# Fewer slots per expert, a down projection with tokens as rows, one relu for two chunks, and a new order, in a routed mixture-of-experts kernel

## The chip, the cores and the metric

The kernel runs on one core of a Trainium2 chip. The metric is the time in device microseconds of one execution; lower is better. Engines are named as in the profile: PE multiplies matrices (PEld is its loading of the stationary operand), DVE is the vector engine, ACT the scalar engine, POOL the general one, SP only starts DMAs. PSUM is the memory that PE writes to; it has eight banks of 512 fp32 columns.

## The reference

The input is 16 sequences of 256 tokens with 128 features, 4096 tokens in all. Four layers follow each other, each added to its input after a layer norm.

```python
x = x + attn_a(layernorm(x), ...)    # its softmax sums to one over keys that v does not depend on:
                                     # what is left is (x @ wv.T + bv) @ wo.T + bo
x = x + ffn(layernorm(x), gate_w, w1, w2)
x = x + attn_b(layernorm(x), ...)    # a selective scan with 16 states
x = x + ffn(layernorm(x), gate_w, w1, w2)
```

The feed-forward layer is a mixture of 8 experts with two chosen for each token:

```python
gate_logits = x @ gate_w
top_vals, top_idx = jax.lax.top_k(gate_logits, 2)
top_w = softmax(top_vals)
h = relu(einsum('td,edf->etf', x, w1))          # d = 128, f = 512
expert_out = einsum('etf,efd->etd', h, w2)
final = sum of the two chosen experts' rows, weighted by top_w
```

All data are fp32.

## The kernel before

The tokens are cut into eight blocks of 512. For each of the two feed-forward layers the blocks are grouped in sets: `FIRST` is block 0, block 1, and the pairs 2-3, 4-5 and 6-7; `SECOND` is the pairs 0-1, 2-3 and 4-5, then 6 and 7 alone. A set is routed (`route`, L1133): each chosen row is scaled by its weight and written by an indirect DMA on POOL (`scatter`, L851) to a slot in DRAM that belongs to its expert. `SLOTS` (L32) says how many slots an expert has: in layer 1 192 for a single block and 330 for a pair, in layer 2 216 and 384. If some expert gets more rows than that, a flag is set and the function `general` computes everything again after the main part, without routing.

`experts` (L1183) then works through the eight experts of a set, one tile each. A tile of N slots is C times K rows, C = 2 for single blocks and C = 3 for pairs. For each tile:

- SP fetches the rows (`xs`), PE transposes them in C products against `ident`, and a copy on ACT or DVE brings them to SBUF as `xsT`, 128 features by N tokens.
- Up: four products with chunks of `w1` as the stationary operand and `xsT` streaming, N columns each, into PSUM banks of the kind "b". For single blocks two chunks share a bank (`pair`) and one relu takes both to `h`; for pairs each chunk has a bank and a relu of its own.
- Down: four products with chunks of `w2` stationary and `h` streaming, N columns each, summed in the one bank of the kind "y" (`py`). The result has features as rows. It is copied out (`yT`), transposed back by PE in C products into a "b" bank, copied out again (`yr`) and written to DRAM (`ys`).

`collect` (L1230) gathers the two rows of each token with indirect DMAs on POOL (`gather`, L863) and adds them. Behind layer 1 `mixer` (L1274) computes the selective scan for one or two blocks at a time. It puts its broadcast products into PSUM banks of the kind "B", each as wide as two banks, in which DVE also works in place. `BANKS` (L48) divides the eight banks: five "b", one "y" and one "B" (which counts twice).

All of this is first noted as jobs in a `Plan`. `Plan.forward` places the jobs one by one on the engines by assumed durations; a job that can run on ACT or DVE goes where it starts first, and among jobs that could start at the same time a rank decides, which is read from the string `ORDER`. The instructions are issued in the resulting order, so each engine's queue is fixed in advance and is worked off strictly in that order.

Where the plan has PE idle before a job, the kernel puts idle products there, on a block of zeros (L1488, named ps_y<-blank,ones_d in the profile): one for each 0.24 us of planned idle time, unless a sum in the "y" bank is under way (`summing`). They write to columns of the "y" bank that the tiles do not use. `WARM` limits them to jobs that start before a given time; at 1e6 all jobs do.

Most operations are recorded by one helper, so they have its line, L752, in the profile and are told apart by their tiles. In the profile `w_s` stands for both expert weights: ps_b<-xsT,w_s is an up product, ps_y<-h,w_s a down product. An fp32 product leaves two records, a transpose or a bf16 product one.

Of the kernel before, what the change touches and what calls it, by code (L numbers as in the profile page):

```python
# [19 lines left out]
P = 128  # L20
L = 256
TB = 512
# [9 lines left out]
SLOTS = ((192, 330, 480, 632), (216, 384, 600, 800))  # L32
# [3 lines left out]
WARM = 1e6  # L36
# [11 lines left out]
BANKS = dict(b=5, y=1, B=1)  # L48

ORDER = (  # L50
    "c-l=@2Ow4N8$RdUd&!70vKq1ql~8D@C{dE^GTPA|XlN%R<0l~`5)BE}Pef!SDI=1MG^Bx$k&1iI_<!Gbu73Zn?!D*SZ@l00KJW8B"
    "=S$_1jb!(<qPM-{q&;qMY=SG3cUzS|l8Uq$KUFJ5{S?3EP+zs^os@%5+Gjc2Nq>t9JMzFH%-zB#Ja4nYlf+G$9mW!_B}u0Tn@;cy"
    "9=$jIA+D3ZPjji7tiV5OuUk;*?O$*8qLrzu-V$N+=g3<+pZ`!Jx9QgD!1?BB)t9awRXc6A>8lL0BHpk?^H9z0Zq9<&1B#*wt}!bF"
    "<MdrQn+&dtG+zEKcE);Je%;`<#9N1QgKD&G6_YFD^(u8neD7yjo>LELnfk;)O7lpdNYUauW!dKG>eDNej5Y_9Tyiaar{|HlPdVx1"
    "PKim`3Ho`%YwSAe65bcO&C1KJSbgmZaVW0nprAi2K0QifduD!wxIRy^gfd;<aY1p~l5Ix~f6Cn)_6)Q$+&g1N<iWx9ev_<3>(Z^>"
    "b>*4(&bE;XZ17OM5`N?SvH|f;AC{ghnRM!M_o`iAJDrOo?;iGgR`739>V@?(YHpR&o(~HwuRK>OTlvWEORwX&ROZ4m3(e2o$_wcq"
    "C(fFT?by&g_r`8n@46kO3InGCiZ(6zGbUwj*XwfMM^THv{JhJ|>xpA3lV6SzAK9WE-LCNF&I;Fi-H`)}8YGt)R7R#68HdDV+Sbip"
    "`RkdKktpZu_ZLnF$9ErYa)=(;>a!<#`HbR2j#;gr4y}xzUlXsNbm<j6P$k(vH~1>w`<Bk+HgDszOUF*{R6jCD=G8SHs_EF0fVZ`2"
    "-66f-6Q>?M5*jxxyko8RO{Zx--;y#?>eNCKoOQn`|E|+B<e#5WsuHa4{b-E?SDrjmN*PgQ+H3M0eO5_67`k<=wy_}U$4Y&El=ovT"
    "I&#qVK+h%XFQxzHZ?WJEmU+~c4uq)Xo_E{)=+n(HyV8pLy0xWbdGlJu)3<B%+@GcBJbvc=G(T&}X~&vH<n9N!Hq33G&|`aet~ygC"  # L60
    "ni9HTK;^S(Pjk~LXDUA{A);*6oSX;E?HaK^7U^m9$wfs@3nC43))gfYV>8{}99nMt>)fBdhE?}-)3iz^YcJFInEkx^aCiLUm0ItX"
    "|8rc~$XdJE>Z80uM&g)63&~lPi+370RcjbaoD6h7FnoPXrb(yW-Q$e)&`VLS^jJF;QzP?-;a62#PaL{Xv9$X9w+}bE;_F2tcUlKL"
    "v^*esrGMGn$4uIZ%8%C*zI-bFR9RW96t3dhW<G5NcVYj_Wr|Hd{%Pf>{~I!y8&E#0`IFAVWj-^$=Vs52ob2hgYLKs%-)$V6<g(*s"
    "RsMJFt*4Lf{}r22=}7!E|NLv+JUV#qL-SL7>pkV<3Wpm%&KB$&mVYdNQla3qme{kSizatgOeBWvzb_nfZsSD3Th7v_LsvB06pbzP"
    "xaDU(YO)-=y)KvNO1-=0vZ$64t1SM0M#A<spXes^7S{PDG@g8akt>T&UFq8qc;Vuor0a5Ok0Qh+$9q{9D>q5l&94n_9y(n9D8-=8"
    "bz*9q+t#q18{I!#+U;X;9COOQu4lLILe0f5gFWiU4&gE8Ez)Y&hsSwl9ZNF}<&h?LaNX{%Rgds<Iol?v=WpwO5|v>o8ry0U;O=-B"
    "OD>q(x6<XXhKIkOl8(mWe;gd^6?eY;JSlj-p#g2#>#|M!&>{K#>i%^_6V*>%?s13|FU-q1(rkWhO4Gfv+p7*-qheY=J~3^07vVR{"
    "q%06KxgXr<;fve++1YT`BhXG)S>#^a3!mZu9X@Y?&TW798^3;qbbc5SeD-=c+4y(z@(-O7&2c+#N@_olIv8(1^YGWaXGg=TbX8S*"
    "pOi)!@{|U9CYo$<nCtM}vdPpz<sG@fH*n2}_{PBrb98QO%1q1S{cf(V575~c6LKZJaO}AapLd6>mp55Duh004nWwYu=jn2(;+yU}"
    ")t833zENM1P_K8_i}rJHUAOncEc@ujsPwhY_3EMuDq|g0t~=jM4q~>(HknU%Fc@dGC1mkcLWet7)N8+U`h@D~A62FHXi!}(O6~i@"  # L70
    "=C8TY;`O3ac@L-jSmdTO$qujXY)Sl?(fK2LfB!4p=@&Z3<84r3#rDHJvsd2i?B5__=5TtvwEFR54SJRmCZTh@2TkW4Xjgi7<KpgO"
    "PG5>>e3g7-Os1$}?vbO>#*bpABrJB-_(Q#ENZ;_GN+(ETe?(r*bM1F0&0V!54wD}%dX?5kmf41IHcz(<7?^2`zqv9r_FTuEo0)bW"
    "x(B?aHAlXAE67dTyfjv!ciM*Ag<iA2M2z|JSnA)>@#WI}{JcJ$TeZRdwPg!D-R-9KX)0v-`RTM(%H8~$R^_PR@3%BTZHk^@M&6Rp"
    "ts<dyF|LWdeZ}#sF0NM#d#!O*_Dthz<)mEoPiKbf&**Dk`<mZgEwg=J>g;7=bdy#r_qJ&4pjk`+m73Dtzu8H3U#R47*%KWP{c|kD"
    "9nW7?lhFHlzvx2TKfyhB3;uarYg5;e(|$Fqc~WG8t5u9liOLO$+Lo27_F-!Y>4F6d%F}*Kd*-<1nJ9iPp*+Yc@li@|<i1N2V&l?Z"
    "-<nRlS*ge8+qX8_<v*SJL%-rvhi9$z8TXT?a`3d%%8R!ppA&m|J#xwZ33oKg;|E_I=%e=*8$PKCi!nSjJ?_3lfzfU8v%~ao*shr$"
    "45Y7r(dv6&K4){A=-A!FEx-1T%b(H~t5v#B7Wv+mRPN$)DOB$0i=+p3Pdu!qR9LN8``~Q&*6(ulOy#D?2B+iU14}ZQ6<yZdPdK3!"
    "a&Ff`GCPWP8(H(OO_aS;^2=$yjGfNrngsd#RzpiFPxmHvkqa(A9x}9Xm6uW)v7goJJ9u?q_TA))H>Km!9g=dHD1QmbhLT#-`MgA<"
    "Xzv%{yIf4Aj`;9q$;KM+ibCmqEz?`D+N*IFw@(yp7*4ln*g2_uxl*Xl`Or4X>rJ2D)Wk`p{+krEv(GQTxk~QGw6bo8AIa(3iiL&B"
    "?<4D%yfY7xX}>shPrN5vY+8+sAl}Po#K`S=h<D3ex4;+GuMO(#7QYHiKB+X+B{pft^S847=b8h3bw0l<8RHr8q$FEnP5Qk<7IW|J"  # L80
    "y`Hi1_`gOWeNKVPPPfUVWa9<vZa0?n1$C+pF8cJT#zjRzAmiHHv>{2vRof=UeR-FSjfi~ixUA(Q{z3HN+x7jSM_jkvz_lLBNJS6D"
    "C4}93qhFz`DPpRq?_n2iw9P0(XW^aQ#{;X?+N8qTa$C1ZNWH%t!b=g!m3&yd#>VjNg97j8TV_1IQlYxp#A)xP@xAxs_Id~kUoBX5"
    "A+u#(f@W0ooIR%$w`(ud9a@%^yyR<GbMp1ak>xf4St)1VxmC0gmQC|4TEzJEWd}@4$z$1_UngHHv1K$ZR==uj+-&St`Sr>6^p8nJ"
    "GRyW~QJuYSrdYX=rRD@1&47kKRfP_38t;tdXC>;UH#zq`x^UR@WJGCC_z`_eL#10%IrBTpPKwsVh@39lDi>a`r7_`!1ukwD_xXC?"
    "^8T(lm_@DCvGoJBjfxzu!lq|hu@#q@^^F^6_lF<6n_1=M6EUkK+HwBMu-9Qvbt@tq`S!meAL`M3^AkJcr&jdWXm^CH`ZitQZhL;x"
    "whL=>DtbN+tnmtY5ODg8wX#S-nyh(Yhb`AA=SZ}=SwusmbJF@LyCR!o=KRT0dA;OB$30nx*t#upHZ`Xrzl9zQ+u17ND{nvFUh}x@"
    "S$%5QL-O1n`Rq>*B!Zsg7FeoHkSoJma(jo~jKA9Ds!epRw3r#}B1VfZ92>j(ta5N!QG}u~Caxa#r=ir@ct&2*E59(ejS1WZy~WFZ"
    "st?LdnJ|)QrgKWLAzFNgqs7ODpKErhybw<v^VDP3*Sc~$`)0|zB^rel*<~;GoXwWk*HGMh+e}gG;O|?i^%>U%_D>U43Qt~WHXEM6"
    "P3R6K+v@Km$#~{0HpFK+jL+E~=<3E7+21N_X|B7X*wWsU_h7S0<r&ZYZBh%fd|o(})>pmT;`hEfuY2B8g~w5`X(D#pzs>JWOEy3G"
    "<;F_eEgR?LFlUcm%MV#0yLFylWZ$%%_jV_@Txct?dv;D%?t1#~<F$RMt;>HkzwkQX)K;}EZ9$QD`?sJs_oT;M{1pDCMDQSMMeedk"  # L90
    "?qzAN+2s<4>aA9ni>dNc_I^^xsChPdz$-MP?t`xF<2W)P^M#6=-N+8rAI=$ujj`=To4rzd6HG13ou@c=iG9DcT2nOo)9w7_&z9S3"
    "=v*A3W{SH^-jLAxdYXdV*(X&|mIvx{qSasQ-86sE*Gs-7vlLS{)t_$P-{Sh>i?N|@cYDxkeCmQ9k(LHE1?Tr^wth4@JY>aP`!#ql"
    "IABYKN$)d-!{5XX$k^1)JXCgo2-)6MmTUN}wapM;IjrO!I}mij*=hcWMNj9HUv6nfkEBjadhL71CJkGlQI-CdKj+zmAv`nV;?xSF"
    "=;zx@at0>SJ!$7FhwgoiBRPw2IyRb3m~u0!{Zx%vc=(b~0pWdW?XE#<C;#q<tb)d*yi;;Bc8uj%9L(ub+Mj6k#?B?9Dm%zQPN#Iy"
    "f-O4LTFn=ST@2OT{BvG@n^3<_Ki1`Nj&k*MYx(2pKFU#kHNL@of9pX@&(v$>hjDZJvMpaN-v^w!VZBzbim_HyHs~A{|M2UCe3#L<"
    "GdsGK8aW=)Roj2w;TJ2a`H9EK@YeP<&2dSqjC!atRCo8I%c9Rq-FxDrZmGH#Jy7uTXq)%k*CN-g*Y~Y6esEPre4mEv#0ajg)1{;9"
    "Ok&>E?OopxlrqJ1cx#WYyOg4W<GQF{Jej)p*Pg#pi=RjtX?T*6tAA%tty5}$u-LCX-1MpcRngelWfj4q*^i4Wo@Q0J99Pze(_dAX"
    "eq-#8e=R$+cS~*+UwJP?W3~jxVvD;{VbWr|m<tI{6{^fqo1#<gd^+8ZDFwzH`R14GrsyxN)w;BNL?Q9L{o13;AI@!FZflz{G9lOO"
    "rF*B;ddt@{`W)O}S?A~}v=Gw2<iZLj1?UJ2f+pRop4@QcjQ1`3{H<dat4`T-ZI_nLyXxr+YuC-(NZy?lJ$$uG&Cq{e)}{}>(oGMQ"
    "Yq`taug*_W4)#p<)KlG=qG8Xwz9;Hc(1Lii&z|WNuivlI%jnwEqn}?-9m$+|t=u)~r*cB7&&J%`hzC2@h*v%TZT@`symM`C$q8Rf"  # L100
    "%<ih#*xF#HRF69!thVaOoY-+;#^=l@&cwNBv-${monOI^cN&?}uRb1cF?`W`+QGT>d7E_Ud7D!Q{rXmkth>soX}wq=b#zdb$E_Bd"
    "jtd9@{b!Kwm+kqkAd!*zt?`V6-TUc@dz}<o6|5u*l4bvJsXbZ({Z_|5k=Nv~v64i$C_Tgrb8$C|%H6EV*)cC)h7;+{h>T11e?B0k"
    "%vVTDI3f}=Yj)`Z7dhu<kA{Ep3f&tV%q@3kj4Tp0Z11g@D{Ih4gt}1aoCa#0%)~2|Lmh5voaQsScU#r9OvUcR1jedj7{-7Xcn2Ri"
    "fe|D|(gY1|P&h{56pe96hQ=`(qX-U#;RH?5I0FXLU^qjgd2l`$!(cdgLu1jR!as)HfZYXN;}}liI0d$12)GcKzz`H1!U5ZXJGgKH"
    "`oq~};0Ff;M$;e&QIZf46ptApK$J9k!3Y?3Ul=}3z<t0!lAypP+M2`Xk{He5gDn{x4rbu0H2g|{2yhx6j9|cu7#IOJgFnH^;1i4h"
    "GvH4I7%l+g;DNa$h=wFk>;f1B*bL0UF@^wf&<q3#r#S+K;Xphw2rtd0z<m-U2r!ocUr`W3cqoW1Lvb-&0KdRnw5Wi@DF6@xnBssi"
    "!6jH5=g<trgS&#?g#b_l8;=02N)X@}B$tBdf}aIA7bb=T0D!r0Bd`d97@nE|34sZ~afaf6O$opPuoxHu2I2q<uqxP9fHNGN53mCG"
    "fH*O91+qqfW0IICDd6&PoLvy12m*rOF^E7gRFFOdJpdO(1}Ff?z#xPXSPViNk%~ZkA}ID?U=+NMk1`G%kAlI&SiycIj)PQ#RSBBM"
    "P~Zsg9H8O|NC^_)iipT#0Pb)TFbO1y#9<C#o*<}T1b_+VkW14X6h00ECUK1AABD;S@)fK}!N4H%*!Urpa1<E^KXKv@TnQjSViX62"
    "&Ij{BsF1$|%reX-1tR7UfS@pYU}*}#5Az3UA%I6kj6@V+na$FKL0@nbF)h4iP|YC}VX!c3G+T0P{h`XkQ7&0P+4>az7ZxTw1kH|R"  # L110
    "OOA#Nh5Q7`qF`AvkRS})6;KJWUH}q}(nGT`pc;VNu)9N)5iXE&*r*WD1iLMRgaqdz5}=Z05eJabC`gP8K}P7n`h(&F$Og&@q!%aQ"
    "Vk9blhNgHFikrkq4k#@KvJ5A1Buot2nJp2799#789l#Bdg5)FMnE}f=NE9#u2jUBf4^;uk23UrI709B8L$ZLMIA}?D79eI6&1Fvn"
# [102 lines left out]
class Plan:  # L215
# [79 lines left out]
    def forward(self, rank):  # L295
# [33 lines left out]
        for _ in range(n):  # L329
# [38 lines left out]
            for table, s in ((j.after, done + HOP), (j.next, t)):  # L368
                for a in table:
                    when[a] = max(when[a], s)  # L370
                    left[a] -= 1
                    if not left[a]:
                        offer(a)
# [1185 lines left out]
```

## Time and profile before

| | |
|---|---|
| median of 6 runs | 688.06 us (680.34 to 690.06) |
| the profiled execution | 689.38 us |
| its span, first to last instruction | 687.7 us |
| PE busy | 569.8 us, 2928 records |
| DVE, ACT, POOL busy | 331.0, 327.8, 323.7 us |
| mean granted PE clock | 0.919 |
| up and down products | 211.1 and 226.6 us, 640 records each |
| idle products | 71.3 us, 526 records |
| indirect DMAs on POOL | 128 scatters of 980 ns and 128 gathers of 974 ns |
| DMA traffic | 55.09 MB, 80 GB/s on average |

The chain of waits is followed back from the last instruction: at each step to what released it. A line of the groups gives the engine, the operation, what it writes and reads, the shape, the count, then the busy time, the mean of one, and the idle time of the engine before it with what ended it. Matmuls are pipelined: the duration of one record is longer than the distance to the next, so that the cost in a dense stretch is read from one start to the next.

### The profile page before, as it was taken

Reading aid. Unit: us, or ns where it says so; the run is one execution under the profiler, and the core shown is the slowest. Engines: PE = TensorE matmul, PEld = TensorE weight load, DVE = VectorE, ACT = ScalarE, POOL = GpSimd, SP = SyncE. Lnnn points to the kernel's source line nnn. Section 1 sums busy time; section 2 is a strip of 40 time slices with the busy share of each in tenths; the row PEclk is TensorE's granted clock in tenths of the full one; section 3 lists DMA queues with packets and bytes.
Section 4 is the critical chain, followed back from the end, with each engine's and each line's share of the span. In section 5 each row is a group of like instructions: output and inputs, shape, how many; then the busy total and the mean of one; then the engine's idle time right before and its main releaser. Section 6 shows DMA issues by size and latency. Waiting matters only on the chain.

```text
span 687.7 us, 9182 instructions
## 1 busy us (share of the span) xinstructions
PE 569.8 (83%) x2928; PEld 416.6 (61%) x2928; DVE 331.0 (48%) x1073; ACT 327.8 (48%) x795; POOL 323.7 (47%) x451
## 2 busy tenths in 40 slices
PE   7988987686988797969987898998479939887695
PEld 7988976554656474636654454654246626686585
DVE  4736543233577456748766675776253512101010
ACT  1223653333777445748566676874134523343130
POOL 3266154545437456373847384316705563244413
PEclk9999998978999789989999999999779978898799
DMA  8933121322023111321233123202333132232211
GB/s 248 294 119 115 40 66 42 98 75 68 26 86 93 35 44 51 100 69 33 69 99 90 33 66 92 59 28 80 84 89 92 38 101 63 90 95 58 68 61 47
DMA packets 76375, 55.09 MB, mean 80 GB/s; under 512 B 8064, under 2 KB 69152, under 8 KB 76320
## 3 DMA queue, kind: packets, MB, share of 16 engines
q1 hardware_dynamic: 66464, 37.35, 18.6%
q0 software_dynamic: 8192, 16.79, 8.4%
q8 instruction: 25, 0.41, 0.3%
q10 hardware_dynamic: 1664, 0.29, 0.2%
q14 instruction: 30, 0.25, 0.1%
HBM read 27.09 MB, written 27.32 MB: 79 GB/s over the span
## 4 chain that ended last, share of the span: by engine, by line
PE 72%; another core or an unknown queue 8%; ACT 7%; issue 7%; DVE 4%; POOL 0%; DVEq 0%; ACTq 0%; POOLq 0%
PE ps_b L752 40%; PE ps_y L752 23%; PE ps_y L1488 7%; PE ps_B L752 2%; ACT decay L752 1%; ACT h L752 1%; ACT th L752 1%; ACT L752 1%; ACT row L752 1%; DVE w L752 1%; DVE ps_B L752 1%; ACT yr L752 1%; ACT yT L752 0%; DVE xn L752 0%
## 5 line engine op out<-in xcount | busy, mean ns | idle before, releaser
L752 PE MATMUL ps_y<-h,w_s 128*128 128x330 f32 (+3 forms) x640 | 226.6, 450 | 18.2 <-issue 8.7
L752 PE MATMUL ps_b<-xsT,w_s 128*128 128x330 f32 (+3 forms) x640 | 211.1, 449 | 30.8 <-ACT xsT L752 12.6
L863 POOL DMA_INDIRECT yy<-ys,of x128 | 124.7, 974 | 121.9 <-issue 60.9
L851 POOL DMA_INDIRECT slots<-row,to x128 | 125.5, 980 | 103.8 <-issue 32.8
L752 PEld LDWEIGHTS ps_b<-xsT,w_s 128*128 128x128 f32 x640 | 120.3, 206 | 77.0 <-issue 21.1
L752 ACT ACTIVATE h<-ps_b 128x384 f32<-128x384 f32 (+2 forms) x209 | 99.0, 481 | 105.0 <-PE ps_b L752 67.1
L752 PEld LDWEIGHTS ps_y<-h,w_s 128*128 128x128 f32 x640 | 111.9, 205 | 52.6 <-issue 20.1
L1488 PE MATMUL ps_y<-blank,ones_d 128*128 128x128 f32 x526 | 71.3, 287 | 10.8 <-POOL ones_d L752 4.0
L1488 PEld LDWEIGHTS ps_y<-blank,ones_d 128*128 128x128 f32 x526 | 66.0, 200 | 14.6 <-issue 4.5
L752 PE MATMUL ps_b<-ident,yT 128*128 128x128 f32 (+3 forms) x208 | 47.8, 290 | 24.7 <-ACT yT L752 21.6
L752 ACT COPY yT<-ps_y 128x384 f32<-128x384 f32 (+3 forms) x62 | 25.0, 403 | 73.1 <-PE ps_y L752 36.2
L752 POOL TENSOR_TENSOR rstd<-var,root 128x8 f32<-128x8 f32 (+1 forms) x20 | 29.9, 1494 | 54.7 <-DVE var L752 49.6
L752 PEld LDWEIGHTS ps_b<-ident,yT 128*128 128x128 f32 (+3 forms) x208 | 27.3, 143 | 41.3 <-ACT yT L752 25.0
L752 DVE TENSOR_SCALAR h<-ps_b 128x330 f32<-128x330 f32 (+2 forms) x47 | 24.4, 524 | 55.7 <-PE ps_b L752 45.9
L752 ACT COPY yr<-ps_b 110x384 f32<-110x384 f32 (+3 forms) x57 | 24.6, 431 | 50.9 <-PE ps_b L752 31.5
L752 DVE TENSOR_TENSOR ps_B<-du,ps_B 128x224 f32<-128x224 f32 (+15 forms) x55 | 22.0, 400 | 43.8 <-remote 14.0
L752 PE MATMUL ps_b<-ident,xs 110*128 110x110 f32 (+3 forms) x208 | 40.5, 276 | 2.1 <-issue 1.1
L752 ACT ACTIVATE th<-later,lneps,ha_s 128x112 f32<-128x112 f32 (+13 forms) x85 | 39.1, 504 | 0.0
L752 PEld LDWEIGHTS ps_b<-ident,xs 110*128 110x128 f32 (+3 forms) x208 | 28.1, 149 | 13.8 <-issue 6.0
L752 DVE BATCH_NORM_STATS2 stats<-x 128x6 f32<-128x128 f32 x128 | 28.9, 279 | 12.7 <-ACT x L752 12.4
L752 ACT COPY xsT<-ps_b 128x330 f32<-128x330 f32 (+3 forms) x55 | 21.7, 403 | 27.0 <-PE ps_b L752 15.8
L752 DVE COPY yr<-ps_b 128x384 f32<-128x384 f32 (+3 forms) x23 | 11.7, 508 | 47.1 <-PE ps_b L752 21.8
(170 smaller groups left out, 677.5 us busy)
## 6 DMA issues: line engine op xcount, KB each, us to landing
slots<-blank SPq DMA_DIRECT2D x3, 1536.0 KB
xs<-slots SPq DMA_DIRECT2D x24, 192.0 KB
ys<-yr SPq DMA_DIRECT2D x24, 192.0 KB
w_s<-in_w SPq DMA_DIRECT2D x16, 256.0 KB
xs<-slots SPq DMA_DIRECT2D x24, 165.0 KB
ys<-yr SPq DMA_DIRECT2D x24, 165.0 KB
xT<-in_xT SPq DMA_DIRECT2D x8, 256.0 KB
slots<-row,to POOLq DMA_INDIRECT x128
```

The costliest lines, as they stand in the source:

```text
L752: return lambda: f(*[real(x) for x in a], **{n: real(x) for n, x in k.items()})
L851: inst = nc.gpsimd.indirect_dma_start(out=real(out), out_offset=bass.IndirectOffsetOnAxis(ap=real(rows), axis=0), in_=real(in_), in_offset ...
L863: nc.gpsimd.indirect_dma_start(out=real(out), out_offset=None, in_=real(in_), in_offset=bass.IndirectOffsetOnAxis(ap=real(rows), axis=0),)
L1488: nc.tensor.matmul(out=spare, lhsT=ones_d.real(), rhs=blank.real()[:, 0 : TB - NMAX], start=True, stop=True,)
```

## The change

- Slots: in layer 1 single blocks have 176 instead of 192, pairs 330 as before; in layer 2 200 instead of 216, and 360 instead of 384 (K is 120 instead of 128).
- Down projection of pairs (`byrow`): now `h` is the stationary operand, K tokens at a time, and a chunk of `w2` streams, 128 columns. That is 12 products for a tile, four summed for each of three groups of rows. The result has tokens as rows, is copied to `yr` at once and written out; the copy `yT` and the three transposes are gone. Single blocks go on as before.
- Up projection of pairs: two chunks go into the two halves of a "B" bank, and one relu takes both to `h`, 660 or 720 columns.
- Banks: three "b" instead of five, two "B" instead of one.
- Idle products: none in the first 12 us of the plan, none for planned gaps below 0.5 us, and one for each 0.26 us of a gap instead of 0.24. They are 232 instead of 263.
- In the plan a PE job behind another PE job waits no longer for the hand-over time that the plan assumes between engines; down products have a sequence of their own (`turn="y"`).
- A new `ORDER`, so that the queues of all engines are arranged anew.

```diff
-SLOTS = ((192, 330, 480, 632), (216, 384, 600, 800))
+SLOTS = ((176, 330, 474, 628), (200, 360, 532, 704))
...
-WARM = 1e6
+COLD = 12.0
...
-BANKS = dict(b=5, y=1, B=1)
+BANKS = dict(b=3, y=1, B=2)
...
             for table, s in ((j.after, done + HOP), (j.next, t)):
                 for a in table:
-                    when[a] = max(when[a], s)
+                    inner = e == "PE" and table is j.after and "PE" in jobs[a].took
+                    when[a] = max(when[a], done if inner else s)
...
-                idle[i] = start[i] - free if start[i] < WARM else 0.0
+                idle[i] = start[i] - free if start[i] > COLD else 0.0
...
-        pair = 2 * N <= TB
+        byrow = C > 2
...
-                py = bank("y", P, N)
-                yT = new("yT", [P, NMAX], bufs=YT)[:, 0:N]
+                py = bank("y", K, C, P) if byrow else bank("y", P, N)
                 yr = new("yr", [P, CMAX, P], bufs=XS)[0:K, 0:C]
+                if not byrow:
+                    yT = new("yT", [P, TMAX], bufs=YT)[:, 0:N]
...
-                    if pair:
+                    if 2 * N <= TB:
                         ph = bank("b", P, 2, N)
+                    else:
+                        ph = bank("B", P, 2, TB)[:, :, 0:N]
                     for c in (2 * half, 2 * half + 1):
-                        if not pair:
-                            ph = bank("b", P, N)
                         matmul(
-                            ph[:, c % 2] if pair else ph, w1_s[:, e, ts(c, P)], xsT, turn="up",
+                            ph[:, c % 2], w1_s[:, e, ts(c, P)], xsT, turn="up",
                             hold=[h] if c % 2 == 0 else (),
                         )
-                        if not pair:
-                            relu(h[:, c % 2], ph)
-                    if pair:
-                        relu(h, ph)
...
+                    relu(h, ph)
+                if byrow:
+                    for k in range(C):
+                        for c in range(NFC):
+                            matmul(
+                                py[:, k], hs[c // 2][:, c % 2, ts(k, K)],
+                                w2_s[:, e * NFC + c, :], c == 0, c == NFC - 1,
+                                hold=[yr] if c == 0 and k == 0 else (), turn="y",
+                            )
+                    copy(yr, py)
+                else:
...
-        spare, summing = kinds["y"][0][:, NMAX:TB], 0
+        spare, summing = kinds["y"][0][:, TB - P : TB], 0
         for job, way, idle in plan.order():
 
-            for _ in range(0 if summing else int(idle / 0.24)):
+            for _ in range(0 if summing or idle < 0.5 else int(idle / 0.26)):
```

## The prediction

> **What bounds the kernel now.** I read the busy shares first, then the chain of waits, the busy time by stretch, the groups kept apart by shape, the waits and short pieces of the timeline.
>
> ```profile
> PE 569.8 (83%) x2928; PEld 416.6 (61%) x2928; DVE 331.0 (48%) x1073; ACT 327.8 (48%) x795; POOL 323.7 (47%) x451
> PE 72%; another core or an unknown queue 8%; ACT 7%; issue 7%; DVE 4%; POOL 0%; DVEq 0%; ACTq 0%; POOLq 0%
> ```
>
> PE carries 72% of the chain. The stretches show that it is bound in two ways:
>
> ```profile
> 440.00:460.00 20.00, 20.00 (x97) 12.60 (x97) 15.79 (x55) 16.55 (x42) 0.00 (x0) 1.00 0.07 19
> 480.00:500.00 20.00, 8.83 (x36) 4.64 (x34) 4.21 (x9) 1.94 (x4) 15.36 (x19) 0.76 0.28 79
> 552.00:572.00 20.00, 9.35 (x30) 5.29 (x29) 1.60 (x4) 3.50 (x9) 8.87 (x13) 0.67 0.26 75
> ```
>
> After the length come PE, PEld, DVE, ACT and POOL, then the granted clock. Where POOL issues nothing (440 to 460) PE has no gap. Where POOL issues gathers and scatters one after the other, all the compute engines mostly stand, and the clock is 0.76 and 0.67. Dense stretches cost what their products cost; set boundaries cost stalls, most of the 118 us (687.7 less 569.8) in which PE is idle. A shorter product pays in the first kind. The 256 indirect DMAs behind the second kind (974 and 980 ns each on POOL) all stay.
>
> Prices are taken from start to start in dense stretches (an fp32 product leaves two records, a transpose one):
>
> ```profile
> 482.70 0.81 PE L752 MATMUL ps_y<-h,w_s 128*128 128x384 f32 x2
> 483.35 0.81 PE L752 MATMUL ps_b<-xsT,w_s 128*128 128x384 f32 x2
> ```
> ```profile
> 160.40 0.72 PE L752 MATMUL ps_y<-h,w_s 128*128 128x330 f32 x2
> 160.96 0.27 PE L752 MATMUL ps_b<-ident,yT 128*110 128x128 f32 x1
> ```
> ```profile
> 51.10 1.17 PE L752 MATMUL ps_b<-wat,xT 128*128 128x128 f32 x9
> ```
> ```profile
> 128.10 1.14 PE L752 MATMUL ps_b<-xsT,w_s 128*128 128x192 f32 x6
> 129.08 0.81 PE L752 MATMUL ps_y<-h,w_s 128*128 128x192 f32 x4
> ```
>
> So 384 columns take 0.65 us, 330 take 0.56, 192 take 0.98 / 3 = 0.327, about 0.0017 us a column; I put 360 at 0.61. The wat row is the very form of the new down projection: activations are loaded, 128 columns stream, and the loaded operand changes with each product. Nine records take 1.17 us; less 0.27 for the last one that is 0.112 a record, 0.224 a product. Four xs transposes that start at 471.12 are over at 471.56, where the next product starts: 0.11 each.
>
> **The change part by part.**
>
> *Pair tiles, layer 1 (24, width 330 as before).* Removed: four down products and three yT transposes, 4 × 0.56 + 3 × 0.11 = 2.57. Added: 12 × 0.224 = 2.69. PE gets 0.12 × 24 = +2.9 us.
>
> *Pair tiles, layer 2 (24, 384 to 360).* Removed: 8 × 0.65 + 3 × 0.11 = 5.53. Added: 4 × 0.61 + 2.69 = 5.13. −0.40 × 24 = −9.6.
>
> *Single tiles (32, 16 columns fewer).* 8 products × 16 × 0.0017 = −0.22 a tile, −7.0.
>
> Together −13.7 us of PE, in stretches of the dense kind. If a narrow product cost 0.236 (the slower of two wat runs, 16 records in 2.04 us) it would be −6.8; if 0.22, as two transposes, −16.
>
> The Trainium skill ("TensorE: Matmul & The Clock Gate", section "Back-to-back issue gap") speaks against this part: in a stream of weight loads and products it gives some 81 ns at 128 columns against 131 at 512, so that narrow products are dear. By its ratio twelve narrow ones would cost 12 × 81 / (4 × 131) = 1.85 times four wide ones at the least, 4.1 us for 2.24; as an estimate from that page the 48 tiles would then gain 70 us and the kernel would end near 735. The wat row shows no such surcharge at this width, and I go by it.
>
> *The wait for yT in pairs goes.*
>
> ```profile
> L752 PE MATMUL ps_b<-ident,yT 128*128 128x128 f32 x72 | 16.1, 289 | 5.2 <-ACT yT L752 5.2
> L752 PE MATMUL ps_b<-ident,yT 128*110 128x128 f32 x72 | 15.7, 286 | 4.1 <-ACT yT L752 3.9 <-ACT yr L752 0.2
> ```
>
> PE stood 9.1 us before these transposes. The bounds are −9.1 and 0: the 5.2 fall in the gather run of 480 to 500, where ACT itself came late, so the next thing late there is the copy into yr, and PE would meet it at the next down product of the one "y" bank. I take the other row alone, −4.
>
> *One relu for two chunks; no yT copy.*
>
> ```profile
> L752 ACT ACTIVATE h<-ps_b 128x384 f32<-128x384 f32 x110 | 53.2, 489 | 61.2 <-PE ps_b L752 37.5 <-remote 15.8 <-issue 6.2
> L752 ACT ACTIVATE h<-ps_b 128x330 f32<-128x330 f32 x69 | 30.1, 446 | 31.1 <-PE ps_b L752 24.5 <-PE ps_y L752 2.5 <-remote 1.0
> ```
>
> From 330 to 384 a relu grows by 0.8 ns a column, so 660 should take 0.71 us and 720 0.76 (twice 446 is the upper bound, 0.89). A layer 1 tile loses 4 × 0.446 − 2 × 0.71 + 0.436 (yT) = 0.80, a layer 2 tile 4 × 0.489 − 2 × 0.76 + 0.477 = 0.91: 41 us off ACT and DVE together. Both are busy 48% and lie beside PE, so nearly all of it is hidden. What can show is PE's waits for them: 12.6 us for xsT and 4.7 for h of DVE.
>
> ```profile
> PE ps_b L752 <- ACT xsT L752: 12.6, 3, 10.6
> PE ps_y L752 <- DVE h L752: 4.7, 2, 4.5
> ```
>
> The 12.6 are mostly one wait of 10.6, in 552 to 572, where nothing is queued on ACT; it stays. Bounds −17 and 0, taken −4, the h row.
>
> *Idle products.* 263 become 232. Before the first expert product there are 145 and then 118, at the end 61 and 63; both fill waits for DMA chains and cost nothing either way. In between 57 become 51: at 0.223 (97 records in 10.83 us in the chain of waits) −1.3 us.
>
> *No idle product before 12 us.* PE then starts the layer norm chain without a run-up. The first stretch of the old kernel has a clock of 1.00 throughout. At clock 0.5 the chain's first dense piece would double:
>
> ```profile
> 14.15 2.15 PE ps_b L752 x17
> ```
>
> Bounds 0 and +4 (what follows it up to 18 us doubling too); taken +2.2. The Trainium skill (same page, section "What's actually happening") says that the array starts throttled and needs some 3.4 us of steady work; no row here shows a start without it.
>
> *Order and queues.* SP loads two xT blocks ahead of the first weights; slots1 and slots2 are cleared behind all the weights. Their 3 MB and the weights share 37 us at 250 to 280 GB/s before the first scatter (36.6 us), so the sum of bytes ahead of the first fetch hardly moves. POOL now gathers set 0 before it scatters blocks 2 and 3, and scatters both later pairs before it gathers the first. Every indirect DMA is still issued once. Which boundary stalls is not to be read from that. I take 0, bounded by one boundary stall more or less: 9.10 + 5.21 us of PE idle in 480 to 500, ±15.
>
> *Sum.* −13.7 − 4 − 4 − 1.3 + 2.2 = −20.8 against the profiled execution's 689.38 (span 687.7 and 1.7 around it): 668.6. The median of the runs is 1.3 lower, so **667 us**. A difference under 1% is about what a measurement here can't tell from none.
>
> **The rivals.**
>
> *The mixers hold the B banks (slower).* The up products of pairs now take "B" banks, two in all, which the mixers take too. DVE works on ps_B in 55 × 0.370 + 40 × 0.904 + 20 × 0.914 + 20 × 0.902 = 93 us (medians), and for so long one bank is gone; about 17 pair tiles fall in it. With one bank a tile needs two rounds of two products (1.2), a relu (0.75) and hand-overs (0.2): 4.3 us, under the 5.3 that PE needs, so nothing shows. It decides from 0.5 us of delay on: a relu behind one scan (up to 1.08) makes 6.5, and where signals come late as in 480 to 500, some 7.2: 17 × 1.9 = +33. **700 us.** Against it: most relus are on ACT (209 of 256), which runs no scans.
>
> *Hidden anyway (no change).* If only stretches with PE above 18.4 of 20 us pay (10 of 34), the products give −4, the waits re-form at the next signal, and the start costs 2.2: **686 us.** For it: 118 us idle, none touched directly.
>
> *Boundaries shrink too (much faster).* Each pair tile loses three hand-overs between engines, and such hand-overs are what stalls in the runs of gathers. If the two big boundaries (14.3 and 10.6 us of idle PE) lose half and the waits for yT and h go entirely (13.8 where I took 8): 667 − 12 − 6, **649 us.** Against it: gathers and scatters are as many as before.
>
> *It doesn't fit.* If an expert gets more rows than its slots, the general path runs behind it, with over a thousand products of 512 columns: beyond 1,500 us. The reference's routing gives at most 142, 310, 176 and 318 rows for 176, 330, 200 and 360 slots, so under 1%.
>
> **How the numbers follow.** Forecast 0.54, hidden 0.15, boundaries 0.15, banks 0.15, overflow 0.01. Faster by over 1% (below 681) are the forecast nearly whole and the boundaries: 0.67; within 1% 0.17; slower 0.16. The range is 640 to 693: it holds the forecast with its bounds and reaches to both middle cases; most of the bank case lies above it. The forecast's own range is 652 to 684.
>
> **What would show it.** Right: ps_y<-h products of pairs 0.112 a record apart; relus of 720 columns near 0.76 us; PE busy near 550 (569.8 − 13.7 − 31 idle products); no yT in pairs; dense 20 us stretches with more tiles in them. Wrong: PE waiting for a relu or for a B bank in 190 to 510 us (banks), the same busy time saved but as much idle added (hidden), PEld busy from end to end in the down projection (narrow products dear).

## The result and the profile after

The kernel after took 689.48 us (median of 42 runs) against 687.94 us of the kernel before (84 runs): ratio 1.0074, 95% interval [1.0048, 1.01]. The ratio compares the faster executions of each kernel alone, since both kernels vary between 675 and 701 us; over all executions the medians differ by 0.2%. A gain of 3% was forecast, and there is none: if anything a loss, of 0.2 to 0.7%. The execution profiled took 693.71 us.

The page after, busy line and chain of waits by engine:

```profile
PE 556.5 (80%) x3490; PEld 463.9 (67%) x3490; DVE 332.3 (48%) x1065; ACT 297.8 (43%) x675; POOL 314.0 (45%) x432
PE 57%; another core or an unknown queue 17%; issue 9%; ACT 8%; DVE 6%; POOL 1%; DMA 0%; DVEq 0%; ACTq 0%; POOLq 0%
```

PE is busy for 13.3 us less. The prediction had it near 550 us, since 31 idle products go as well; that it is 6.5 us more goes with the clock: PE works for 99.6 us at half its clock here and worked for 76.1 before, which by half of the difference is some 12 us more. And PE stands for 692.0 - 556.5 = 135.5 us where it stood for 117.9, and in the chain "another core or an unknown queue" has gone from 8% to 17%: something that the trace cannot name ends twice as much of the waiting.

The prices of the prediction are found again. The timeline of PE, and the relus among the groups kept apart by shape:

```profile
368.10 0.60 PE L758 MATMUL ps_y<-w_s,h 128*110 128x128 f32 x4
368.54 0.72 PE L758 MATMUL ps_B<-xsT,w_s 128*128 128x330 f32 x2
```
```profile
L758 ACT ACTIVATE h<-ps_B 128x720 f32<-128x720 f32 x43 | 33.1, 769 | 40.2 <-PE ps_B L758 20.3 <-issue 12.0 <-remote 5.9
L758 ACT ACTIVATE h<-ps_B 128x660 f32<-128x660 f32 x33 | 23.7, 722 | 48.7 <-remote 18.8 <-PE ps_B L758 18.1 <-DVE w L758 9.8
```

Four narrow records take 0.44 us from start to start, 0.11 each (predicted 0.112), and the relus 769 and 722 ns (predicted 760 and 710). What changed is the waits. The waits of PE (us in total, times, longest), first the one for yT before the change, then those after it:

```profile
PE ps_b L752 <- ACT yT L752: 21.6, 5, 7.4
```
```profile
PE ps_b L758 <- issue: 27.7, 11, 9.3
PE ps_B L758 <- DVE h L758: 16.0, 4, 5.0
PE ps_B L758 <- ACT h L758: 14.3, 5, 5.1
PE ps_b L758 <- ACT yT L758: 10.8, 4, 5.2
```

The waits for yT are halved, and in their place PE stands 30.3 us for a relu that must free a "B" bank. These are two kinds of products, which the groups keep apart:

```profile
L758 PE MATMUL ps_B<-xsT,w_s 128*128 128x330 f32 (+1 forms) x384 | 141.3, 497 | 25.5 <-DVE h L758 7.4
L758 PE MATMUL ps_B<-pieces,sel 96*128 96x112 bf16 (+15 forms) x170 | 22.9, 247 | 26.0 <-DVE h L758 8.6
```

The up products of pairs (first line) wait 13.4 us of the 30.3, with what ACT's relus cost them; the other 16.9 are the mixers' broadcast products (second line), which now find the relus of pairs in the banks that were theirs alone. Stretches of the same kinds as those shown of before (after the length PE, PEld, DVE, ACT, POOL, the granted clock):

```profile
480.00:500.00 20.00, 13.48 (x81) 10.65 (x80) 9.68 (x22) 8.02 (x22) 12.54 (x23) 0.91 0.21 62
540.00:560.00 20.00, 19.79 (x121) 15.42 (x120) 12.05 (x58) 9.88 (x19) 14.43 (x15) 1.00 0.40 103
...
360.00:380.00 20.00, 20.00 (x118) 14.82 (x118) 13.04 (x52) 13.90 (x24) 3.82 (x3) 1.00 0.22 63
```

Still PE has no gap where POOL issues hardly anything (360 to 380), and PE, ACT and DVE stand for long in many stretches of gathers (480 to 500), though not in all (540 to 560). So the products got cheaper, and the stalls got longer by rather more: 17.6 us against 13.3. The question for the experiments was what the stalls are.

### The profile page after: what moved, and what is told of

It is laid out like the page before. It is cut to its first block, busy times and chain, and to the rows that moved or that the text cites. A ratio compares the mean times of both kernels' runs of the same rounds, so it can differ in the third digit from the quotient of the medians.

```text
span 692.0 us, 10152 instructions
## 1 busy us (share of the span) xinstructions
PE 556.5 (80%) x3490; PEld 463.9 (67%) x3490; DVE 332.3 (48%) x1065; ACT 297.8 (43%) x675; POOL 314.0 (45%) x432
## 4 chain that ended last, share of the span: by engine, by line
PE 57%; another core or an unknown queue 17%; issue 9%; ACT 8%; DVE 6%; POOL 1%; DMA 0%; DVEq 0%; ACTq 0%; POOLq 0%
PE ps_y L758 20%; PE ps_b L758 19%; PE ps_B L758 16%; PE ps_y L1502 2%; ACT th L758 2%; ACT h L758 1%; DVE ps_B L758 1%; ACT decay L758 1%; ACT L758 1%; DVE h L758 1%; POOL slots L857 1%; ACT row L758 1%; DVE w L758 1%; ACT yr L758 1%
## 5 line engine op out<-in xcount | busy, mean ns | idle before, releaser
L758 PEld LDWEIGHTS ps_y<-w_s,h 128*110 128x110 f32 (+1 forms) x1152 | 152.1, 192 | 40.8 <-issue 18.2
L758 PE MATMUL ps_y<-w_s,h 128*110 128x128 f32 (+1 forms) x1152 | 165.8, 289 | 15.1 <-issue 8.3
L758 PE MATMUL ps_B<-xsT,w_s 128*128 128x330 f32 (+1 forms) x384 | 141.3, 497 | 25.5 <-DVE h L758 7.4
L758 PEld LDWEIGHTS ps_B<-xsT,w_s 128*128 128x128 f32 x384 | 70.7, 204 | 56.7 <-issue 13.8
L758 ACT ACTIVATE h<-ps_B 128x720 f32<-128x720 f32 (+1 forms) x76 | 56.8, 749 | 88.9 <-PE ps_B L758 38.4
L758 PE MATMUL ps_y<-h,w_s 128*128 128x176 f32 (+1 forms) x256 | 58.9, 360 | 6.3 <-issue 2.8
L758 PE MATMUL ps_b<-xsT,w_s 128*128 128x176 f32 (+1 forms) x256 | 58.4, 360 | 2.6 <-issue 2.2
L758 PEld LDWEIGHTS ps_y<-h,w_s 128*128 128x128 f32 x256 | 47.0, 215 | 8.9 <-issue 4.1
L758 PEld LDWEIGHTS ps_b<-xsT,w_s 128*128 128x128 f32 x256 | 47.1, 215 | 4.9 <-issue 2.8
L758 PE MATMUL ps_b<-ident,xs 110*128 110x110 f32 (+3 forms) x208 | 38.8, 278 | 14.2 <-issue 13.6
L758 ACT ACTIVATE th<-later,lneps,ha_s 128x112 f32<-128x112 f32 (+14 forms) x85 | 38.9, 503 | 0.0
```

Of the source, the lines that this page charges most:

```text
L758: return lambda: f(*[real(x) for x in a], **{n: real(x) for n, x in k.items()})
```

## The experiments

The kernel before ran beside every experiment. In these later runs, on four chips, its median lay between 551.7 and 553.2 us, not at 688. All ratios below are to that time, with their 95% intervals. It is the largest thing that the experiments found, so it comes first.

Three theories go through the expectations. SIGNALS: PE stands because signals of finished work come late while POOL issues gathers and scatters. CLOCK: PE works more at half its clock, for want of work or idle products that keep the clock up. ORDER: the new sequence costs or brings something by itself. The expectations of a_cold, b_slots, b_plain and a_plain were written when the kernel before was known at 688 us only; their microseconds do not apply at 552.

**The same two kernels in the later runs.** No edit in either.

> The kernel after, unchanged, beside the kernel before on the chip of this call. In the last call the kernel before took 552.58 us where it had taken 687.94, with PE's granted clock at 0.99 instead of 0.92, and the kernel after with the old rule for idle products was at 0.969 of it. Theory SIGNALS: where the clock and the signals are undisturbed (before near 552) the kernel after gains what the prediction's sum gave, ratio 0.962 to 0.975; where before is near 688 again, 1.003 to 1.011 again. Theory CLOCK (the gain of the last call was due to the old rule for idle products): ratio 0.99 to 1.01 in both.

> The kernel before, unchanged, for its trace on the chip of this call. If the 118 us in which PE stood in the profiled execution before the change belong to the kernel (dependences at the set boundaries), they are found again here: PE idle 100 us or more, some 33 gaps over 1 us. Theory SIGNALS (they belong to the late signals of that execution): PE idle under 35 us, fewer than 8 gaps over 1 us, the granted clock at 0.98 or more, and the products as many and as long as there.

Measured: before 552.57 us, after 538.21 us, ratio 0.9738 [0.9717, 0.9758]. The same instructions gain 2.6% here and gained nothing there. Both results are those of theory SIGNALS. The busy lines and chains of b_same and of a_same:

```profile
PE 526.7 (96%) x2928; PEld 394.7 (72%) x2928; DVE 331.9 (60%) x1073; ACT 329.6 (60%) x795; POOL 323.0 (59%) x451
PE 84%; ACT 5%; POOL 3%; DVE 2%; issue 2%; DMA 2%; POOLq 0%; DVEq 0%
```
```profile
PE 505.2 (94%) x3490; PEld 429.3 (80%) x3490; DVE 335.1 (62%) x1065; ACT 298.5 (56%) x675; POOL 314.8 (59%) x432
PE 74%; DVE 5%; ACT 3%; DMA 3%; issue 2%; POOL 2%; SPq 0%; POOLq 0%; DVEq 0%; ACTq 0%
```

Counts, and the busy time of DVE, ACT and POOL, are those of the recorded executions within 1%; the unknown queue is gone from the chain. PE stands for 550.6 - 526.7 = 23.9 us and for 536.4 - 505.2 = 31.2 us. Of the gaps over 1 us that had held PE 33 and 36 times, five are left in each.

One place shows what makes them. The timeline of the kernel after, recorded execution (rows of other work left out):

```profile
152.01 0.45 PE L758 MATMUL ps_b<-ident,xs 110*128 110x110 f32 x3
152.08 0.96 POOL L869 DMA_INDIRECT yy<-ys,of  x1 [0.30 <-issue]
...
159.69 0.95 POOL L869 DMA_INDIRECT yy<-ys,of  x1 [0.30 <-issue]
160.95 0.95 POOL L869 DMA_INDIRECT yy<-ys,of  x1 [0.30 <-issue]
161.75 0.79 SPq L758 DMA_DIRECT2D xs<-slots  x1
161.75 0.43 ACT L758 COPY xsT<-ps_b 128x330 f32<-128x330 f32 x1 [9.68 <-remote]
```

And the same instructions in a_same:

```profile
125.65 0.45 PE L758 MATMUL ps_b<-ident,xs 110*128 110x110 f32 x3
125.70 0.96 POOL L869 DMA_INDIRECT yy<-ys,of  x1 [0.30 <-issue]
...
126.13 3.14 SPq L758 DMA_DIRECT2D xs<-slots  x2
126.13 0.43 ACT L758 COPY xsT<-ps_b 128x330 f32<-128x330 f32 x1 [0.44 <-PE ps_b L758]
```

The transposes end 0.45 us after they start in both. Here ACT takes the result 0.03 us later; there 9.29 us later, and SP's next fetch goes out at the same moment as ACT starts. Meanwhile POOL issues its indirect DMAs 1.25 to 1.30 us apart in both. ACT and SP wait for the same semaphore, which PE updates, and the trace has that update at 161.73 us, in a_same 0.01 us after the transposes' end. So the signal of PE's end is late. Whether the results are late with it can't be told, because the ends of products in the profile are modelled.

Over the whole traces, 70 updates of PE's semaphore come more than 0.8 us (up to 10.1) after the last end of a product that makes them in the recorded before, and 75 (up to 9.3) in the recorded after; in b_same and a_same there is none (updates in the last 8 us, when the program ends, are left out). No update of ACT or DVE that the traces hold is so late in any of the four. Of the gaps over 1 us, 22 of 33 with 77.5 of 94.7 us hold such a late update in the recorded before, and 29 of 36 with 96.4 of 109.5 us in the recorded after.

The recorded traces also lack records: they hold 2311 (before) and 2051 (after) updates that do not come from DMAs, where b_same and a_same hold 2753 and 2421, and half as many from DMAs. So it is open whether the taking of the trace had a part in the lateness.

What the recorded executions lost against the later ones, with the clock records of the traces laid over PE's busy time (half of the time at half clock is counted as lost, which is an estimate):

| us | before | after |
|---|---|---|
| PE idle, recorded less later run | 117.9 - 23.9 = 94.0 | 135.5 - 31.2 = 104.3 |
| PE busy at half clock, recorded and later | 76.1 and 3.4 | 99.6 and 4.5 |
| lost by that, half of the difference | 36.4 | 47.6 |
| together | 130.4 | 151.9 |
| of a difference of the spans | 137.1 | 155.6 |

Why PE's signals came late in the recorded runs and not in the later ones (another chip, something else that ran beside them, or the recording itself) no trace says. It stays open.

**Idle products.**

```diff
-                idle[i] = start[i] - free if start[i] > COLD else 0.0
+                idle[i] = start[i] - free if start[i] > 4.0 else 0.0
...
-            for _ in range(0 if summing or idle < 0.5 else int(idle / 0.26)):
+            for _ in range(0 if summing else int(idle / 0.24)):
```

> The kernel after with the old rule for idle products: they start at 4 us of the plan instead of 12, every idle time counts (not from 0.5 us on) and one idle product stands for 0.24 us instead of 0.26. Theory CLOCK: the cold start cost 2 to 4 us and the missing idle products 2 to 8 more, so 681 to 690, ratio to before 0.990 to 1.003, and the busy time under the low clock falls from 99.6 us towards 85. Theory SIGNALS and theory ORDER: at most the cold start, 689 to 693, ratio 1.002 to 1.008.

Measured: 535.34 us, 0.9692 [0.9666, 0.9718], 2.9 us under the kernel after (538.21). So the old rule for idle products brings a little, in the direction of theory CLOCK. The start of PE in a_same, then in a_cold:

```profile
11.29 2.50 PE L758 MATMUL ps_b<-wat,xT 128*128 128x128 f32 x10 [0.38 <-DVE wat L758]
...
14.43 1.49 PE L758 MATMUL ps_b<-wat,xT 128*128 128x128 f32 x6
```
```profile
11.60 1.38 PE L758 MATMUL ps_b<-wat,xT 128*128 128x128 f32 x10
...
13.27 0.83 PE L758 MATMUL ps_b<-wat,xT 128*128 128x128 f32 x6
```

Without a run-up the same products take 0.25 us a record, with one 0.12: 1.12 + 0.66 = 1.8 us, where the prediction took 2.2. The clock records agree: the first one, with the full clock granted, begins at 9.7 us in a_cold and at 16.0 in a_same. Before that the windows show 1.00 in both for want of a record, so a 1.00 in the first stretch does not by itself rule out a cold start.

**Slots alone.** `SLOTS` as in the change, in the kernel before; in b_slots2 with an order searched on from before's own at the new widths (a search that shifts ranks and keeps what shortens the plan).

> The kernel before with the new numbers of slots alone (176 for 192 in layer 1, 180 for 192 a tile in layer 2); its own order and everything else stay. By the prediction's prices PE has 32 x 0.22 + 24 x 0.32 = 14.7 us less to do. If products pay as the prediction had it and the new order is what ate the gain (theory ORDER): 673 us, ratio 0.979. If the time is set by the runs of gathers and scatters, in which signals come late and PE finds the same idle time again (theory SIGNALS): less than a third of it, 683 to 688, ratio 0.993 to 1.000, with PE's busy time down by 13 to 15 and its idle time up by 9 or more. If shorter dense stretches leave the clock at half speed more often (theory CLOCK): in between, about 680, with more busy time under the low clock than the 76 us of before.

> The kernel before with the new numbers of slots, and before's own order searched on at the new widths (at these widths the order on file left PE waiting: 1518 records of idle products where before has 526). By the prediction's prices PE has 14.7 us less to do: 538 us, ratio 0.973. If the slots are worth what the kernel after lost without them (539.79 against 538.21): 551, ratio 0.997. Theory ORDER: near 1.00, since the sequence is still the old one.

b_slots took 658.41 us, 1.191 [1.1886, 1.1934], and none of the theories had that. Idle products among the groups of its page:

```profile
L1488 PE MATMUL ps_y<-blank,ones_d 128*128 128x128 f32 x1518 | 189.0, 281 | 14.0 <-ACT yT L752 7.1
```

Three times as many idle products as before (526 records) stand for waiting that the plan itself has. The likely reason is that the ranks fit the durations for which they were found, and that other durations send the planner down another path. The run tells nothing on slots. b_slots2 does: 543.13 us, 0.9834 [0.9811, 0.9856], 9.6 us less, between the two values expected; what the search alone brought is in it.

**Order.** Only the string `ORDER` differs from the kernel named, taken over job by job from the other kernel and searched on.

> The kernel before with only its order changed: the order of the kernel after, carried over instruction by instruction and searched on from there; slots, structure of the pairs and idle rule are those of before. Theory ORDER: the new sequence alone gains what the kernel after with the old sequence lost (553.09 against 538.21, 0.027): ratio 0.965 to 0.98. If the order is worth nothing by itself: 0.995 to 1.01.

> The kernel after with an order taken over from the kernel before, instruction by instruction, and searched on from there: the set boundaries come in before's sequence. Theory ORDER (the new sequence is worth or costs something by itself): over 1.5% away from the kernel after, to either side. If the order is worth nothing, as the prediction took it: within 1% of the kernel after (0.96 to 0.98 of before, where before is near 552).

b_order: 549.16 us, 0.9935 [0.9911, 0.9958], -3.6 us. a_old: 553.09 us, 1.0019 [0.9998, 1.0041], 14.9 us over the kernel after. So what an order is worth depends on the durations and banks around it: carried into before, the new sequence brings a quarter of what its loss costs after.

**Slots and order without the structure, and the structure without the slots.**

> The kernel before (pairs down-project with slots as columns, a relu for each chunk, five banks b and one B, idle products from the start) with the new numbers of slots and an order taken over from the kernel after and searched on from there. By the prediction's prices the structure of the pairs is worth 0.12 - 0.11 x 24 = +2.9 us for layer 1 and (2.69 - 4 x 0.61 - 0.33) x 24 = -1.9 for layer 2, so about nothing on PE: the rest is slots and order, and this kernel is within 1% of the kernel after (0.965 to 0.98 of before, where before is near 552). If one relu for two chunks and the missing yT are what pays: 0.99 to 1.00 of before.

> The kernel after with the old numbers of slots (192, 330; 216, 384) and an order that was searched anew for them from the new one, since the order on file makes the planner run out of buffers at these widths. What is left of the change is the structure of the pairs, the idle rule and an order of the new kind. By the prediction's prices PE has 14.7 us more to do than in the kernel after: 0.027 more in the ratio (some 0.99 to 1.00 of before, where before is near 552). If the slots do not matter (other engines or the mixers set the pace there): within 0.008 of the kernel after.

(Layer 1 in the expectation of b_new is 0.12 x 24 = +2.9.) b_new: 536.51 us, 0.9701 [0.968, 0.9722]: the old pairs with new slots and order are no slower than the kernel after. a_wide: 539.79 us, 0.9764 [0.9742, 0.9786], only 1.6 us over it, where 14.7 was priced. So beside the new slots and order the structure of the pairs brings nothing that shows. Beside the old slots it does: a_wide is 9.4 us under b_order, which has the old slots and structure and the new kind of order. Against b_order (549.16) the slots alone (b_new) bring 12.7 us, the structure alone (a_wide) 9.4 and both (the kernel after) 11.0, so the two do not add. That spoke for a cost hidden inside the structure.

**The banks.** The narrow down products of after with the banks of before:

```diff
-BANKS = dict(b=3, y=1, B=2)
+BANKS = dict(b=5, y=1, B=1)
...
-                    else:
-                        ph = bank("B", P, 2, TB)[:, :, 0:N]
                     for c in (2 * half, 2 * half + 1):
+                        if 2 * N > TB:
+                            ph = bank("b", P, N)
...
-                    relu(h, ph)
+                        if 2 * N > TB:
+                            relu(h[:, c % 2], ph)
+                    if 2 * N <= TB:
+                        relu(h, ph)
```

> The kernel after with the banks of before (five b, one B): the up products of pairs take a b bank for each chunk of d_ff, with a relu for each; the narrow down products, the slots and the idle rule are those of after, and the order was searched on from after's. ACT and DVE get 96 relus more (48 pair tiles with four instead of two), 48 x 0.2 = 10 us. If the B banks cost nothing while signals are on time: 534 to 540, ratio 0.966 to 0.977. If they do (mixers hold the B banks): under 533, below 0.965.

Measured: 522.34 us, 0.9459 [0.9432, 0.9486], 15.9 us under the kernel after, and the fastest kernel of all. Its busy line:

```profile
PE 492.8 (95%) x3448; PEld 422.1 (81%) x3448; DVE 334.8 (64%) x1084; ACT 304.3 (58%) x748; POOL 316.4 (61%) x436
```

Its order was searched on as well; that alone, on the kernel after with the old idle rule, is worth 1.1 us:

> The kernel after with the old rule for idle products and with its own order searched on. The old rule alone gave 535.34 (0.9692). If the order on file is still worth improving by its plan: 532 to 535, ratio 0.963 to 0.968; if the plan no longer tells orders apart at this level: 535 to 538, 0.968 to 0.974.

a_best: 534.2 us, 0.9676 [0.9652, 0.9701], against 535.34, a difference within the intervals. So some 15 us are the division of the banks together with the joint relu. No run parts the mixers' hold on the "B" banks from three "b" banks instead of five, or from the relu for two chunks. Against a_same PE stands 3.1 us less, has 21 idle products less (4.7 us of planned waiting) and works 4.1 us less at half clock (some 2 us); the rest, some 6 us, is spread over its products.

**Plain DMAs for indirect ones.** All 256 indirect DMAs became plain ones of the same size on SP's queue, with rows at fixed places.

```diff
-            inst = nc.gpsimd.indirect_dma_start(
-                out=real(out), out_offset=bass.IndirectOffsetOnAxis(ap=real(rows), axis=0),
-                in_=real(in_), in_offset=None, **kw,
-            )
+            nc.sync.dma_start(out=real(out)[P * c : P * (c + 1)], in_=real(in_))
```

> The kernel before with each of its 256 indirect DMAs replaced by a plain DMA of the same size on SP's queue, at the same place of the order: rows go to and come from fixed places instead of those that the routing names, so the choice of slots is left out of the data, and POOL issues no DMA. Theory SIGNALS: nearly all of PE's idle time in the runs of gathers and scatters (104 of 118 us) goes, and the clock rises with it: 570 to 610 us, ratio 0.83 to 0.89. Theory ORDER: those waits are made by the dependences at the set boundaries and not by POOL's issuing, so most stay: 650 to 690, ratio 0.945 to 1.00.

> The same replacement in the kernel after: 256 plain DMAs on SP's queue for the indirect ones on POOL's, rows at fixed places. Theory SIGNALS: without the late signals the cheaper products show, so this kernel is 12 to 25 us under the other one with plain DMAs (some 555 to 590, ratio to before 0.81 to 0.86). Theory ORDER: the new order's own waits stay, and this one is within 1% of the other or above it. Banks shared with the mixers: PE waits for ps_B banks grow in this kernel alone, and it is slower than the other one.

With other rows the flag behind the main part is set, and `general` computes everything again: 2990.15 and 2970.29 us. The main part is still to be read: its last output starts at 542.5 us in b_plain and at 521.9 in a_plain, against 545.8 and 529.9 with indirect DMAs in b_same and a_same. As a test of late signals it came to nothing, since there were none here to remove. It shows that with signals on time the 256 indirect DMAs cost 3 to 8 us more than plain ones do.

**A stand-in for late signals.** Eight copies on ACT and eight on DVE at every fourth indirect DMA:

```diff
+            if way[0] == "POOL" and way[1] == 1.26:
+                issued += 1
+                for _ in range(8 if issued % 4 == 0 else 0):
+                    nc.scalar.copy(late_a, late_a)
+                    nc.vector.tensor_copy(late_d, late_d)
```

> The kernel before with eight copies of 128 columns on ACT and eight on DVE (about 2 us on each) in their streams at every fourth indirect DMA, 64 times in all, as a stand-in for late signals. If all of it were exposed it would cost 64 x 2.2 = 140 us. ACT and DVE are busy 60%, so a part is hidden: 590 to 650 us, ratio 1.07 to 1.18, with PE idle 30 to 90 us more and part of PE's work under the low clock.

> The kernel after with the same copies at every fourth indirect DMA. If the kernel after is dearer to delay (as in the recorded runs, where it lost 16 us more), it loses its 14 us here too: within 1% of b_late or above it. If delays of ACT and DVE cost both the same, it stays 10 to 18 us under b_late, and the recorded difference has another cause than delays of these two engines.

> The old structure of the pairs with the new slots and the new kind of order (undelayed 536.51, ratio 0.970), with the same copies. If the structure (banks shared with the mixers, one relu for two chunks, one y bank held for twelve products) is what is dear to delay: at least 8 us under a_late. If it is the new order: as slow as a_late, within 5 us.

> The kernel after with the old rule for idle products and its order searched on (undelayed 534.2, ratio 0.968), with the same copies. If the low clock after each delay is a good part of the loss and idle products hold it off: 5 us or more under a_late, with less busy time under the low clock. If idle products placed by the plan's own idle times miss the delays: 4 us under a_late, as without delays.

> r_banks with the eight copies on ACT and DVE at every fourth indirect DMA, as in a_late. If the B banks and the joint relu are what is dear to delay: it loses about what the old structure lost (102), so 7 us or more under a_late (below 640, ratio below 1.157). If the y bank held for twelve narrow products is: it loses 108 or more, as a_late.

| kernel | with delays, us | ratio, interval | ratio without | cost of the delays |
|---|---|---|---|---|
| before (b_late) | 659.05 | 1.19 [1.1847, 1.1953] | 1 | 0.190 |
| after (a_late) | 647.16 | 1.1686 [1.1644, 1.1729] | 0.9738 | 0.195 |
| b_new (n_late) | 638.45 | 1.1523 [1.1473, 1.1573] | 0.9701 | 0.182 |
| a_best (g_late) | 644.87 | 1.1642 [1.1569, 1.1716] | 0.9676 | 0.197 |
| r_banks (r_late) | 626.47 | 1.1346 [1.131, 1.1383] | 0.9459 | 0.189 |

The delays cost 101 to 109 us, each known to some 3 or 4 us. The kernel after keeps most of its gain (11.9 us under b_late). So delays of ACT and DVE at these places do not by themselves turn the gain into a loss. In the recorded runs it was PE's signals that came late, so the stand-in is not that condition itself. b_new is 0.0126 or 7 us cheaper to delay than the kernel after, with its new structure; but before, whose structure is the same as that of b_new, is only 0.005 cheaper, and r_late 0.006, which the intervals do not tell from nothing. The expectation of b_late was missed: its delays cost more than the 650 us at its upper end. One wait does stand where the banks would have it. Waits of PE in a_late, then in r_late:

```profile
PE ps_B L758 <- ACT h L758: 15.5, 8, 3.1
```
```profile
PE ps_b L758 <- ACT h L758: 6.1, 5, 3.1
```

In a_same no such wait is in the list. Denser idle products (g_late) gain 2.3 us, no more than without delays, so there is no sign that they hold off the low clock after a delay; with an interval of some 4 us more can't be said.

## Why the prediction was wrong

*The step that failed* is the first reading, "set boundaries cost stalls", and with it the terms of the sum that price PE's waits: -4 for yT, -4 for h, and 0 for "Order and queues" with one stall either way. Together they had PE stand 8 us less; it stood 17.6 us more (135.5 against 117.9), and that is more than its busy time fell. The 118 us were taken for a property of the boundaries that the change leaves as it is. Most of them (94.0) are not found in the same kernel when PE's signals come on time: it stands for 23.9 us then. The lines that hinted at it were in the profile: 8% of the chain with an unknown releaser, and on ACT relus waiting 15.8 us for "remote". In the recorded condition the kernel after lost 151.9 us to standing and half clock where the one before lost 130.4, by one trace of each. This is the rival *hidden anyway* in its mechanism (same busy time saved, as much idle time added), at 0.15, and its price of 686 was near. Its reason was not quite right: the idle time did not stay, it grew.

*What makes the kernel after lose more in that condition* (16 us, by which its gain of 14.4 becomes a loss) stays open. The recorded waits for "B" banks (30.3 us) point at the banks, but a_late does not lose its gain, the stand-in delays other engines than the one whose signals were late, and no later run brought the recorded condition back.

*The sum* can be held against the runs without late signals, where -14.4 us came out of -20.8:

| term | predicted | measured in the later runs |
|---|---|---|
| slots | -14.7 | -9.6 in before (b_slots2), -1.6 in after (against a_wide) |
| order | 0 | -3.6 alone (b_order), -6.6 on top of the slots (b_new) |
| idle products and start | -1.3 + 2.2 | +2.9 (after less a_cold) |
| pairs: products, yT, relu | +2.9 - 1.9 - 4 - 4 = -7.0 | after less b_new +1.7, less the idle rule -1.2; a_wide less b_order -9.4, less the idle rule -12.3 |

The prediction added terms that do not add: slots and structure each pay, and the second pays little beside the first. That the total comes as near as it does is partly luck, since the slots brought less than priced and the order, put at nothing, 3.6 to 6.6 us.

PE's own work fell as priced: 526.7 - 505.2 = 21.5 us, of which 31 idle products at 0.223 us make 6.9 and the rest 14.6 (predicted 13.7). The Trainium skill ("TensorE: Matmul & The Clock Gate", "Back-to-back issue gap") would have made narrow products dear; at 0.11 us a record the trace after shows no surcharge, so choosing the row over the rule was right. The same page ("What's actually happening") gives some 3.4 us of steady work for the run-up; in a_same the products run at half speed from 11.29 us and the full clock is on record from 16.0, so it took 4.7 us here.

*Banks.* The rival *mixers hold the B banks* stood at 0.15 with a price of +33 and a threshold of 0.5 us of delay, below which "nothing shows". "Nothing shows" is wrong: with signals on time the new division of the banks, with the joint relu, costs some 15 us by r_banks. That the mixers' hold is what costs is not shown. The waits behind it are short, and part of them is planned and filled with idle products, so the list of PE's waits hardly shows them. Without that cost the narrow products and the missing yT seem to bring more than they were given: r_banks, which has no joint relu and the dearer idle rule, is 14.2 us under b_new, where the terms of the pairs gave -7.0. Each of the two has an order of its own, so that is not theirs alone.

*Relus.* ACT and DVE lost 329.6 + 331.9 - 298.5 - 335.1 = 27.9 us, not 41. No run shows what they bring by themselves; r_banks, which has twice the relus for pairs, is the faster one.

## What to carry to other kernels

Before an idle time is priced, look at who ends it: "remote", "unknown queue" or a wait whose producer ended microseconds ago is longer than the kernel's own dependences make it, and its size need not stay when the order changes. An order that was searched for is part of the durations and the buffers it was searched with; an edit beside it is judged only with an order of its own. When a change takes buffers from one user to give them to another, measure it with and without that part: here it took away half of what the rest brought (15.9 of some 30 us).

## What the runs showed of the hardware

- The same kernel took 688 us in the recorded runs and 551.7 to 553.2 us in the later ones on four chips, with the same 256 indirect DMAs at the same pace on POOL. In the recorded trace 70 updates of PE's semaphore came up to 10.1 us after the modelled end of the products (75, up to 9.3, in the kernel after), in the later traces none, and none of ACT or DVE that the traces hold was so late. PE's mean granted clock was 0.919 instead of 0.995.
- Products that start without a run-up take 0.25 us a record instead of 0.12, here from 11.29 to 16.0 us. The granted clock in the windows reads 1.00 there because the trace has no clock record before 16.0.
